# A graph layer's gather: fewer, wider register loads on SyncE, and more source columns copied by VectorE and ScalarE

## The chip, the cores and the metric

The kernel runs on one core of a Trainium2 chip. The metric is the device time of one execution in microseconds; what is compared is the median of several.

## The reference

A layer of a graph network with 12,500 nodes of 48 features and 400,000 edges, sorted by their destination. Every edge's message goes through two dense layers, and the messages are summed by destination:

```python
h = jnp.maximum(_layernorm(x, axis=-1), 0.0)
x_i, x_j = h[dst], h[src]
tmp = jnp.concatenate([x_i, x_j, edge_attr], axis=1)      # 48 + 48 + 32
hid = jax.nn.relu(tmp @ W1 + b1)                          # 128 wide
msg = hid @ W2 + b2
out = x + jax.ops.segment_sum(msg, dst, num_segments=12500)
```

All of it is in float32.

## The kernel before

A first part of some 70 us normalizes the nodes and multiplies them with the two halves of `W1`. That gives two tables with one row of 128 numbers for each node: `tab_a` for the destination (with the bias) and `tab_b` for the source, both in HBM. `tab_b` is also kept in SBUF, transposed, as `bt`: there a node is a column.

The edges are then worked off in 391 chunks of 1024, each of 8 tiles of 128 edges. For each chunk TensorE adds up, in PSUM (`pre`), the destination's row, the edge's attributes and the source's row. The first two come from one matmul per tile (line 409): since the edges are sorted, a chunk's destinations lie in a short run of nodes, so the left factor `lhs` holds a 0/1 matrix, which VectorE makes with one comparison (line 387, with a sum that goes to `deg` and is read out by a second instruction), and the right factor `rhs` holds the run's rows of `tab_a`. ScalarE then applies the ReLU (line 446, one activation a chunk, called `hid`). A second set of matmuls (line 456) sums the hidden values by destination, with the 0/1 matrix `hot` that VectorE makes (line 398), and VectorE adds the sums to a window of destinations, `seg` (line 471). Now and then the window moves on: VectorE clears and copies it (lines 487 and 489), and the old one is multiplied with `W2` and stored.

What bears on the change is how the source's rows get into `pre`. They can't be had by a comparison, since sources are random. There are three ways, and each of the 3125 tiles goes by one of them:

- By an indirect DMA of GpSimd, one instruction for each tile (line 379), from `tab_b` into `gb`, which has eight buffers of a chunk each. GpSimd starts with them before the loop and runs ahead as far as the buffers allow.
- By rows: SyncE reads the numbers of sources into its registers and issues one small DMA for each row (line 293). `RPART` = 15 rows a chunk make a tile in some eight and a half chunks.
- By columns: VectorE and ScalarE read numbers into their registers and copy one column of `bt` at a time into a tile `gt` (line 352), 128 instructions for a tile. TensorE multiplies such a tile by the identity and so turns it (line 430).

`PARTS` divides a chunk's columns into groups, each with its engine, its place in the strip `cols` of numbers and its size. The groups stand at fixed places of each engine's order: on VectorE the first follows the comparison of line 387, then come the second, the addition of line 471, the third, the comparison of line 398, and the fourth and fifth. For each group the engine first reads all its numbers by one register load (`numbers`, line 276), rounded up to a multiple of four, and then issues the copies. The second group's load also brings the address at which line 471 adds (`PLACE`). `tiles_of` works out how many tiles the columns make in all; the tiles that go by columns are not gathered by GpSimd.

SyncE's order in a chunk (`prepare`) is: the edges' attributes (line 362), the destinations (line 364), a register load of 16 numbers from `last` (the first destination, `BASE`, and 15 sources), the rows of `tab_a` (line 372) and the fifteen small DMAs of line 293.

Of the kernel before, what the change touches and what calls it, by code (L numbers as in the profile page):

```python
# [24 lines left out]
NCH = (NT + T - 1) // T  # L25
# [29 lines left out]
ROWS0 = 3  # L55
# [1 line left out]


PARTS = (
    (True, 0, 8), (True, 8, 15), (True, 24, 16), (True, 40, 20), (True, 60, 12),  # L60
    (False, 72, 12), (False, 84, 8), (False, 92, 8), (False, 100, 20), (False, 120, 12),
    (False, 132, 12),
)
PLACE = 23
STRIP = 144
PART = sum(n for _, _, n in PARTS)
SLOT = [at + k for _, at, n in PARTS for k in range(n)]
FIRST_OF = [sum(n for _, _, n in PARTS[:k]) for k in range(len(PARTS))]
RPART = 15
BASE = 0  # L70

BT0 = 16512
SEG0 = 165792
SEG_SIZE = 8 * L


AT_PLACE, AT_SEG, SEG, NEXT = 16, 17, 18, 19
WIDTH = 20
SLOTS = (NCH + 2 + P - 1) // P
BANK = 4  # L80

# [147 lines left out]
def windows(nc, tc, gp, bt, ident, idx, raw, rhss, x_t, tab_a, tab_b, dst, edge_t, w2s, b2s,  # L229
# [5 lines left out]
    with ExitStack() as es:  # L235
# [26 lines left out]
        st = {}  # L262
        gts = {}
        gss = {}

        def group(c):

            g = max(0, sum(first <= c for first in BEGINS) - 1)
            return g, c - BEGINS[g]
# [4 lines left out]
        def numbers(c, at, n, engine, table=last):  # L274

            return nc.values_load_multi_w_load_instructions(  # L276
                table[c % P : c % P + 1, c // P, at : at + n],
                engines=[engine], min_val=0, max_val=1 << 23,
                skip_runtime_bounds_check_because="numbers of nodes, and what is made of them",
            )[1]  # L280
# [48 lines left out]
        def columns(c, part):  # L329
# [5 lines left out]
            copy = nc.vector.tensor_copy if dve else nc.scalar.copy  # L335
            place = PLACE if at < PLACE <= at + PARTS[part][2] and c >= 2 else None
            size = -(-n // 4) * 4 if place is None else place + 1 - at
# [16 lines left out]
        def span(c):  # L354

            return next(w for w, last in SPANS if c < last)

        def prepare(c):
            n, w = min(T, NT - c * T), span(c)
            at = c * CE  # L360
            lhs = lhss[c % 3]
            nc.sync.dma_start(lhs[W:K, : n * P], edge_t[:, at : at + n * P])
            row = ld.tile([W, CE], I16, name="row")
            nc.sync.dma_start(
                row[:w, : n * P],
                dst[at : at + n * P].rearrange("(o e) -> o e", o=1).to_broadcast([w, n * P]),
            )
            m = max(0, min(RPART, len(BYROWS) * P - (c - ROWS0) * RPART)) if c >= ROWS0 else 0
            base, *nodes = numbers(c, BASE, 1 + m, mybir.EngineType.SP)
            rhs = rhss[c % 3]  # L370
            base = base.with_bounds(min_val=0, max_val=4 * HID * (N - 1))
            nc.sync.dma_start(
                rhs.bitcast(U8)[:w, :],
                taba8[bass.ds(base, 4 * HID * w)].rearrange("(w h) -> w h", w=w),
            )
            st[c] = dict(n=n, rows=nodes)
            gb = gp.tile([P, T, HID], F32, name="gb") if c >= RAW else None
            for t in range(n - len(COLS_OF.get(c, ())) - (c in BYROWS) if c >= RAW else 0):
                nc.gpsimd.indirect_dma_start(  # L379
                    out=gb[:, t, :], out_offset=None, in_=tab_b[:, :],  # L380
                    in_offset=bass.IndirectOffsetOnAxis(
                        ap=srci[:, c * T + t : c * T + t + 1], axis=0
                    ),
                )

            deg = degs[c % 3]
            nc.vector.tensor_scalar(  # L387
                lhs[:w, : n * P], row[:w, : n * P], bw[:w, c : c + 1], None,
                op0=ALU.is_equal, op1=ALU.add, accum_out=deg[:w, :1],
            )  # L390
            st[c].update(rhs=rhs, lhs=lhs, gb=gb, deg=deg)
# [70 lines left out]
        def add(c):  # L462

            s, w = st.pop(c), span(c)
            k = group(c)[0] % 2
            of = SEG0 + k * SEG_SIZE
            at = s["base"].with_bounds(
# [44 lines left out]
        with tc.manual_schedule():  # L512
            for c in range(NCH + 2):
                g, k = group(c - 2)
                if c < NCH:
                    prepare(c)
                    rows(c, st[c].pop("rows"))
# [173 lines left out]
def tile_gnn_preln(  # L691
# [31 lines left out]
    first = ctx.enter_context(tc.tile_pool(name="first", bufs=1))  # L723
# [28 lines left out]
    flag = const.tile([1, 1], I32, name="flag")  # L752
    last = const.tile([P, SLOTS, WIDTH], I32, name="last")
    cols = const.tile([P, SLOTS, STRIP], I32, name="cols")

# [7 lines left out]
    with tc.tile_pool(name="keep", bufs=1) as keep, tc.tile_pool(  # L763
# [82 lines left out]
        def check():  # L846

            p_c = ps_c.tile([1, P], F32, name="p_c")
            nc.tensor.transpose(p_c, furthest, ident)
            out_of = keep.tile([1, 1], F32, name="out_of")  # L850
            nc.vector.tensor_reduce(out_of, p_c, AX.X, ALU.max)
            nc.vector.tensor_scalar(flag, out_of, 0.5, None, op0=ALU.is_gt)

            nc.vector.tensor_scalar(bw, b0f[:W, :], wcol[:W, :], None, op0=ALU.add)

            nc.vector.tensor_scalar(cols, cols, 4, BT0, op0=ALU.mult, op1=ALU.add)
            rows_at = slice(BASE, BASE + 1 + RPART)
            nc.vector.tensor_scalar(
                last[:, :, rows_at], last[:, :, rows_at], 4 * HID, None, op0=ALU.mult
            )  # L860
            nc.vector.tensor_tensor(
                last[:, :, NEXT : NEXT + 1], last[:, :, NEXT : NEXT + 1],
                last[:, :, SEG : SEG + 1], op=ALU.subtract,
            )
            at = last[:, :, AT_PLACE : AT_PLACE + 1]
            nc.vector.scalar_tensor_tensor(
                at, last[:, :, AT_SEG : AT_SEG + 1], -4.0, at, op0=ALU.mult, op1=ALU.add
            )
            at_place = slice(PLACE, PLACE + 1)
            nc.vector.scalar_tensor_tensor(  # L870
                cols[:, :, at_place], cols[:, :, at_place], 1.0, at, op0=ALU.mult, op1=ALU.add
            )

        b0f = keep.tile([P, NCH], F32, name="b0f")
        node_tables(nc, tc, keep, x, ident, w1, b1, wb, ht, xg, ones, tab_a, tab_b, index, loads,
                    squares, most, check)
    outside = nc.values_load(flag[:1, :1], min_val=0, max_val=1)

    with tc.If(outside == 0) as cmp:
        windows(nc, tc, gp, bt, ident, (srci, rel, bw, wrow, last, cols, degs), (xg, wb, ht), rhss,  # L880
                x_t, tab_a, tab_b, dst16, edge_t, w2s, b2s, sources, out_t)
# [78 lines left out]
```

## Time and profile before

| | |
|---|---|
| median of 3 runs | 3349.78 us (3347.76 to 3354.19) |
| the profiled execution's own time | 3348.55 us |
| its span, first to last instruction | 3346.8 us |
| mean granted TensorE clock | 0.875 |
| tiles by GpSimd, by columns, by rows | 2650 (32 of them raw node rows before the loop), 430, 45 |

In the page's groups a row reads: line, engine, operation, what it writes and reads, count; then busy time in us and mean ns of one; then the idle time of the engine just before these instructions and what ended it. "issue" is idle time in which the engine waited for nothing that the profile shows. A row of a line's own view gives count, the shortest, median and longest duration in ns, and the first and last start. A row by stretches gives the stretch, its length, the engine's busy time with the count in brackets, the granted clock, the DMA share and GB/s. A row of the waits gives who waited for whom, us in total, times, and the longest. A row of the timeline gives start, duration, engine, line and operation, with the idle time before it in brackets. Register loads are done by an engine's sequencer (DVEq, SPq, ACTq) and do not count as busy time of the engine.

### The profile page before, as it was taken

Reading aid. Unit: us, or ns where it says so; the run is one execution under the profiler, and the core shown is the slowest. Engines: PE = TensorE matmul, PEld = TensorE weight load, DVE = VectorE, ACT = ScalarE, POOL = GpSimd, SP = SyncE. Lnnn points to the kernel's source line nnn. Section 1 sums busy time; section 2 is a strip of 40 time slices with the busy share of each in tenths; the row PEclk is TensorE's granted clock in tenths of the full one; section 3 lists DMA queues with packets and bytes.
Section 4 is the critical chain, followed back from the end, with each engine's and each line's share of the span. In section 5 each row is a group of like instructions: output and inputs, shape, how many; then the busy total and the mean of one; then the engine's idle time right before and its main releaser. Section 6 shows DMA issues by size and latency. Waiting matters only on the chain.

```text
span 3346.8 us, 114800 instructions
## 1 busy us (share of the span) xinstructions
PE 2804.1 (84%) x16242; PEld 2228.4 (67%) x16242; DVE 2608.9 (78%) x29052; ACT 3044.9 (91%) x28183; POOL 2516.1 (75%) x2672
## 2 busy tenths in 40 slices
PE   7988888888888888888888888888877888788877
PEld 6676767666666676766666676666665666666655
DVE  6477777777777777788777777887878788888886
ACT  5799999999999998999999999999999999999997
POOL 7777777777777777777777777777777777777776
PEclk9988888888888888888888888998989888899898
DMA  7322223233333333333333333333333333333332
GB/s 259 110 77 78 77 77 78 76 80 83 84 83 82 83 82 83 84 89 88 86 86 88 87 88 85 93 91 93 93 93 93 93 90 93 96 100 98 100 98 76
DMA packets 171145, 307.66 MB, mean 92 GB/s; under 512 B 68611, under 2 KB 93813, under 8 KB 169093
## 3 DMA queue, kind: packets, MB, share of 16 engines
q0 software_dynamic: 84800, 172.53, 20.7%
q1 hardware_dynamic: 85170, 127.53, 12.7%
q14 instruction: 634, 5.19, 0.5%
q8 instruction: 137, 2.24, 0.3%
q10 hardware_dynamic: 404, 0.17, 0.0%
HBM read 284.21 MB, written 18.34 MB: 90 GB/s over the span
## 4 chain that ended last, share of the span: by engine, by line
DVE 34%; POOL 25%; issue 22%; PE 10%; ACT 4%; DMA 3%; DVEq 2%; ACTq 0%; SPq 0%; POOLq 0%
POOL gb L379 25%; DVE gt L352 25%; DVE lhs L387 6%; ACT gt L352 3%; DMA gb<-tab_b,srci 3%; PE pre L409 3%; PE pre L430 2%; PE p_g L456 2%; DVE hot L398 2%; DVEq L276 2%; PE p_n L194 1%; ACT hid L446 1%; DVE seg L471 1%; PE pre L306 0%; ACTq L276 0%
## 5 line engine op out<-in xcount | busy, mean ns | idle before, releaser
L379 POOL DMA_INDIRECT gb<-tab_b,srci x2618 | 2476.4, 946 | 805.3 <-issue 759.8
L352 ACT COPY gt<-bt 128x1 f32 x27705 | 2619.5, 188 | 76.6 <-issue 66.1
L352 DVE COPY gt<-bt 128x1 f32 x27335 | 1839.8, 143 | 616.7 <-issue 578.7
L430 PE MATMUL pre<-gb,ident 128*128 128x512 f32 (+2 forms) x1548 | 851.7, 668 | 234.9 <-DMA gb<-tab_b,srci 227.7
L409 PEld LDWEIGHTS pre<-rhs,lhs 112*128 112x128 f32 x6250 | 888.6, 220 | 187.0 <-issue 118.4
L409 PE MATMUL pre<-rhs,lhs 112*128 112x128 f32 x6250 | 884.3, 302 | 27.5 <-issue 17.1
L456 PE MATMUL p_g<-hot,hid 128*128 128x64 f32 (+4 forms) x6250 | 789.9, 279 | 111.2 <-ACT hid L446 109.2
L456 PEld LDWEIGHTS p_g<-hot,hid 128*128 128x128 f32 x6250 | 769.0, 200 | 139.7 <-ACT hid L446 138.8
L430 PEld LDWEIGHTS pre<-gb,ident 128*128 128x128 f32 x1548 | 314.3, 234 | 536.1 <-issue 469.0
L446 ACT ACTIVATE hid<-pre 128x1024 f32<-128x1024 f32 x391 | 397.7, 1017 | 175.4 <-PE pre L430 158.5
L387 DVE TENSOR_SCALAR_CACHE_REDUCE lhs<-row,bw 64x1024 f32<-64x1024 int16 (+4 forms) x391 | 492.2, 1259 | 3.0 <-DMA row<-in_dst 3.0
L430 PE MATMUL pre<-ident,gt 128*128 128x128 f32 x860 | 224.2, 349 | 137.9 <-DVE gt L352 118.8
L430 PEld LDWEIGHTS pre<-ident,gt 128*128 128x128 f32 x860 | 148.6, 217 | 157.6 <-issue 77.6
L398 DVE TENSOR_TENSOR hot<-wnum,rel 128x512 f32<-128x512 f32 (+4 forms) x391 | 207.0, 529 | 0.0
L459 PE MATMUL p_g<-ident,deg 80*128 80x32 f32 (+4 forms) x782 | 159.7, 286 | 0.0
L471 DVE TENSOR_TENSOR seg<-seg,p_g 128x128 f32 (+4 forms) x391 | 94.1, 241 | 80.6 <-PE p_g L459 79.9
L459 PEld LDWEIGHTS p_g<-ident,deg 80*128 80x128 f32 x782 | 128.3, 206 | 0.0
L499 PE MATMUL p_f<-seg,w2s 128*48 128x512 f32 (+1 forms) x58 | 35.9, 705 | 5.5 <-DVE xseg L506 5.1
L773 POOL DMA_INDIRECT xg<-in_x,srci x32 | 31.0, 967 | 10.2 <-issue 8.8
L500 PE MATMUL p_f<-seg,b2s 1*48 1x512 f32 (+1 forms) x58 | 33.3, 656 | 0.0
L203 ACT COPY tab<-p_n 128x512 f32<-128x512 f32 x33 | 18.7, 584 | 12.1 <-PE p_n L194 11.8
L387 DVE DVE_READ_ACCUMULATOR lhs<-row,bw 64x1 f32 (+4 forms) x391 | 28.8, 74 | 0.0
(78 smaller groups left out, 357.7 us busy)
## 6 DMA issues: line engine op xcount, KB each, us to landing
gs<-tab_b SPq DMA_DIRECT2D x5760, 0.5 KB
lhs<-in_edge_t SPq DMA_DIRECT2D x390, 128.0 KB
gb<-tab_b,srci POOLq DMA_INDIRECT x2618
row<-in_dst SPq DMA_DIRECT2D x90, 128.0 KB
row<-in_dst SPq DMA_DIRECT2D x85, 96.0 KB
row<-in_dst SPq DMA_DIRECT2D x50, 160.0 KB
row<-in_dst SPq DMA_DIRECT2D x87, 64.0 KB
tab_b<-tab SPq DMA_DIRECT2D x3, 1280.0 KB
```

The lines of the kernel that those rows point to most:

```text
L276: return nc.values_load_multi_w_load_instructions(table[c % P : c % P + 1, c // P, at : at + n], engines=[engine], min_val=0, max_val=1 << 23,
L352: copy(gts[j][:, e : e + 1], bt8[:, bass.ds(of, 4)].bitcast(F32))
L379: nc.gpsimd.indirect_dma_start(out=gb[:, t, :], out_offset=None, in_=tab_b[:, :], in_offset=bass.IndirectOffsetOnAxis(ap=srci[:, c * T + t ...
L387: nc.vector.tensor_scalar(lhs[:w, : n * P], row[:w, : n * P], bw[:w, c : c + 1], None, op0=ALU.is_equal, op1=ALU.add, accum_out=deg[:w, :1],)
L398: nc.vector.tensor_tensor(hot[:, :n, :], wnum[:, :w].unsqueeze(1).to_broadcast([P, n, w]), rel[:, c * T : c * T + n].unsqueeze(2).to_broad ...
L409: nc.tensor.matmul(pre[:, t, :], s["lhs"][:K, t * P : (t + 1) * P], s["rhs"][:K, :], start=t % BANK == 0, stop=False, skip_group_check=True,)
L430: nc.tensor.matmul(pre[:, t:e, :], lhsT, rhs, start=False, stop=True, skip_group_check=True)
L446: nc.scalar.activation(h[:, :n, :], s["pre"][:, :n, :], AF.Relu)
L456: nc.tensor.matmul(p_g[:, 0, :], s["h"][:, t, :], s["hot"][:, t, :], start=t == 0, stop=t == n - 1)
L459: nc.tensor.matmul(p_g[:, 1, :], s["deg"], ident[:W, :w], start=True, stop=True)
L471: nc.vector.tensor_add(to, to, s["p_g"])
L499: nc.tensor.matmul(p_f[:, :n], w2s, seg[:, 0, s], start=True, stop=False)
```

## The change

VectorE's groups are 12, 15, 16, 20 and 9 columns instead of 8, 15, 16, 20 and 12, one column more in all (72 for 71). ScalarE's last group is 14 instead of 12 (74 for 72). Together 146 columns a chunk are copied instead of 143. SyncE loads 32 numbers (two chunks' 15 sources and two first destinations) in every even chunk, and uses the second half in the next one. The strips become wider to match.

```diff
 PARTS = (
-    (True, 0, 8), (True, 8, 15), (True, 24, 16), (True, 40, 20), (True, 60, 12),
-    (False, 72, 12), (False, 84, 8), (False, 92, 8), (False, 100, 20), (False, 120, 12),
-    (False, 132, 12),
+    (True, 0, 12), (True, 12, 15), (True, 28, 16), (True, 44, 20), (True, 64, 9),
+    (False, 76, 12), (False, 88, 8), (False, 96, 8), (False, 104, 20), (False, 124, 12),
+    (False, 136, 14),
 )
-PLACE = 23
-STRIP = 144
+PLACE = 27
+STRIP = 152
...
-BASE = 0
+BASE = 2 * RPART
...
-AT_PLACE, AT_SEG, SEG, NEXT = 16, 17, 18, 19
-WIDTH = 20
+AT_PLACE, AT_SEG, SEG, NEXT = 32, 33, 34, 35
+WIDTH = 36
...
+        ahead = []
...
-            base, *nodes = numbers(c, BASE, 1 + m, mybir.EngineType.SP)
+            if c % 2 == 0:
+                ahead[:] = numbers(c, 0, 2 * RPART + 2, mybir.EngineType.SP)
+            base, nodes = ahead[BASE + c % 2], ahead[c % 2 * RPART :][:m]
...
-            rows_at = slice(BASE, BASE + 1 + RPART)
+            rows_at = slice(0, BASE + 2)
```

More of the change, by code (lines that the diff above doesn't have):

```diff
@@ L69 @@
 RPART = 15
-BASE = 0
+BASE = 2 * RPART
 BT0 = 16512
-SEG0 = 165792
+SEG0 = 166176
 SEG_SIZE = 8 * L
-AT_PLACE, AT_SEG, SEG, NEXT = 16, 17, 18, 19
-WIDTH = 20
+AT_PLACE, AT_SEG, SEG, NEXT = 32, 33, 34, 35
+WIDTH = 36
 SLOTS = (NCH + 2 + P - 1) // P
@@ L908 @@
     numbers[2 : NCH + 2, AT_PLACE] = SEG0 + of % 2 * SEG_SIZE - BT0
-    numbers[:NCH, BASE] = first
+    bases = np.pad(first, (0, -NCH % 2)).reshape(-1, 2)
+    numbers[: NCH + NCH % 2 : 2, BASE : BASE + 2] = bases
     numbers[:NCH, SEG] = seg
@@ L920 @@
     rows = by_tile[in_rows].reshape(-1)
-    rows = np.pad(rows, (0, -len(rows) % RPART)).reshape(-1, RPART)
-    numbers[ROWS0 : ROWS0 + len(rows), BASE + 1 : BASE + 1 + RPART] = rows
+    by_chunk = np.zeros((NCH + NCH % 2) * RPART, np.int32)
+    by_chunk[ROWS0 * RPART : ROWS0 * RPART + len(rows)] = rows
+    numbers[: NCH + NCH % 2 : 2, : 2 * RPART] = by_chunk.reshape(-1, 2 * RPART)
     last = np.ascontiguousarray(numbers.reshape(SLOTS, P, WIDTH).transpose(1, 0, 2))
```

## The prediction

> **What bounds the kernel now.** I read the page first: busy shares, then the costliest groups.
>
> ```profile
> PE 2804.1 (84%) x16242; PEld 2228.4 (67%) x16242; DVE 2608.9 (78%) x29052; ACT 3044.9 (91%) x28183; POOL 2516.1 (75%) x2672
> ...
> L379 POOL DMA_INDIRECT gb<-tab_b,srci x2618 | 2476.4, 946 | 805.3 <-issue 759.8
> L352 ACT COPY gt<-bt 128x1 f32 x27705 | 2619.5, 188 | 76.6 <-issue 66.1
> L352 DVE COPY gt<-bt 128x1 f32 x27335 | 1839.8, 143 | 616.7 <-issue 578.7
> ```
>
> By busy share ScalarE is the fullest engine and GpSimd the emptiest. That is misleading: GpSimd's idle time is nearly all "issue", it waits for nobody. So I asked next for the GpSimd gathers (line 379) by stretches, and for where they begin and end.
>
> ```profile
> 200.00:700.00 500.00, 377.71 (x402) 0.86 0.30 77
> 700.00:1500.00 800.00, 604.84 (x641) 0.85 0.32 83
> 1500.00:2500.00 1000.00, 756.41 (x800) 0.87 0.34 89
> 2500.00:3300.00 800.00, 605.14 (x640) 0.90 0.36 96
> ```
>
> ```profile
> L379 POOL DMA_INDIRECT gb<-tab_b,srci x2618: 940/944/1774, 52.6 to 3331.6; - x187
> ```
>
> The counts say one gather per 1.25 us in every stretch (800/641, 1000/800, 800/640), from 52.6 to 3331.6: 2618 x 1.25 = 3272 of these 3279 us. GpSimd never stops. It gathers 2618/387 = 6.76 tiles per chunk, 8.44 us. Now the pace of the chunks themselves, by ScalarE's one activation per chunk (line 446) in the same stretches:
>
> ```profile
> 200.00:700.00 500.00, 63.02 (x62) 0.86 0.30 77
> 700.00:1500.00 800.00, 99.65 (x98) 0.85 0.32 83
> 1500.00:2500.00 1000.00, 120.18 (x118) 0.87 0.34 89
> 2500.00:3300.00 800.00, 96.81 (x95) 0.90 0.36 96
> ```
>
> Up to 1500 us a chunk takes 8.06 to 8.16 us, less than GpSimd's 8.44: the chunks catch up with a lead that GpSimd has from starting at 52.6. From 1500 on a chunk takes 8.42 to 8.47, GpSimd's own pace. The waits say the same. Below are TensorE's longest wait before 1500 and after, then VectorE's wait for TensorE's sums, before and after:
>
> ```profile
> PE pre L430 <- DVE gt L352: 82.2, 79, 2.7
> ```
>
> ```profile
> PE pre L430 <- DMA gb<-tab_b,srci: 227.7, 150, 3.4
> ```
>
> ```profile
> DVE seg L471 <- PE p_g L459: 3.0, 1, 3.0
> ```
>
> ```profile
> DVE seg L471 <- PE p_g L459: 49.4, 27, 4.4
> ```
>
> Early, TensorE waits for VectorE's copied columns and VectorE for nobody: VectorE sets the 8.1 us. Late, TensorE waits for gathers and VectorE idles 49.4 us in all. So GpSimd sets the end, and VectorE is a close second with some 50 us to spare. What fills VectorE's 8.1 us is not its 78% of busy time. Its register loads (line 276) and the timeline of one chunk show it:
>
> ```profile
> L276 DVEq TENSOR_LOAD <-cols x1: 1101/1101/1101, 401.7 to 401.7; - x1
> L276 DVEq TENSOR_LOAD <-cols x1: 1351/1351/1351, 403.4 to 403.4; - x1
> L276 DVEq TENSOR_LOAD <-cols x1: 846/846/846, 405.4 to 405.4; - x1
> L276 DVEq TENSOR_LOAD <-cols x1: 596/596/596, 406.8 to 406.8; - x1
> L276 DVEq TENSOR_LOAD <-cols x1: 1100/1100/1100, 407.7 to 407.7; - x1
> L276 DVEq TENSOR_LOAD <-cols x1: 1107/1107/1107, 409.4 to 409.4; - x1
> ```
>
> ```profile
> 402.02 0.18 DVE L471 TENSOR_TENSOR seg<-seg,p_g 128x32 f32 x1
> 402.84 1.06 DVE L352 COPY gt<-bt 128x1 f32 x16 [0.64 <-issue]
> 403.82 0.28 DVE L398 TENSOR_TENSOR hot<-wnum,rel 128x128 f32<-128x128 f32 x1
> 404.80 1.30 DVE L352 COPY gt<-bt 128x1 f32 x20 [0.69 <-issue]
> 406.34 0.82 DVE L352 COPY gt<-bt 128x1 f32 x12 [0.24 <-issue]
> 407.07 1.26 DVE L387 TENSOR_SCALAR_CACHE_REDUCE lhs<-row,bw 16x1024 f32<-16x1024 int16 x1
> 408.27 0.07 DVE L387 DVE_READ_ACCUMULATOR lhs<-row,bw 16x1 f32 x1
> ```
>
> The five loads are those for 16, 20, 12, 8 and 16 numbers: 0.85 - 0.60 = 0.25 us for four numbers. From 401.7 to 409.4 is 7.7 us; the loads hold the sequencer for 5.0 of them, and the other 2.7 go to sending out some 76 instructions, 0.036 each. (After the load that ends at 402.80 the next starts at 403.4: 0.6 us for sixteen copies and the comparison.) The sequencer is never free: it is the resource, and the "issue" idle of line 352 is its loads.
>
> **The change part by part.** *GpSimd.* 146 columns a chunk for 143 make 385 x 146 / 128 = 439 tiles by column instead of 430, so nine gathers go: 9 x 1.25 = 11.2 us, all of it on the path that sets the end now.
>
> *ScalarE* gets two copies: 2619.5 / 27705 = 0.095 us each, 0.19 a chunk, 73 us over 385 chunks, and four more numbers in its last load, about 0.25 by VectorE's rows, sent while earlier copies still run. What hides it:
>
> ```profile
> ACT hid L446 <- PE pre L430: 158.5, 141, 9.8
> ```
>
> ScalarE waits 158.5 us for TensorE; 73 fit. If that cover were gone, up to 73 + 385 x 0.25 = 169 us could show; below nothing it cannot go. I take 0.
>
> *TensorE* multiplies nine more tiles in single form:
>
> ```profile
> L430 PE MATMUL pre<-ident,gt 128*128 128x128 f32 x860 | 224.2, 349 | 137.9 <-DVE gt L352 118.8
> ```
>
> Two of 0.35 us a tile make 6 us at most, beside its waits: 0.
>
> *SyncE* now loads 32 numbers in every second chunk for 16 in each.
>
> ```profile
> L276 SPq TENSOR_LOAD <-last x421: 275/1192/1482, 76.0 to 3330.4; - x141
> ```
>
> ```profile
> SPq L362 <- PE pre L409: 127.2, 83, 5.3
> ```
>
> No row has a load of 32. It lies between 1.19 (the median, nearly all of them for 16) and 2.38 (twice that); from 0.275 for one number to 1.19 for 16 is 0.061 a number, which gives 2.17, the value I take. So SyncE saves 0.1 us a chunk, and in even chunks the rows behind the load (line 372's and the fifteen of line 293) go out 1 us later, in odd ones 1.2 earlier. SyncE waits 127.2 us for buffers that TensorE still reads, so it runs ahead as far as these allow, and neither shows: 0. Uncovered, 1 us in 196 even chunks would be 196 us. The wider strips make two scalings before the loop longer, by 32 and 64 elements a partition; line 398 does 128 in 0.28 us, so under 0.3 us once.
>
> *VectorE.* Loads grow from 8+16+16+20+12 numbers to 12+16+16+20+12, since nine are rounded up to twelve: +0.25 us. One more copy is sent: +0.04. That is 0.29 a chunk on the engine that has none to spare. The new order adds to it. Count from the end of the last group's load (405.4 + 0.846 = 406.25). Now: twelve copies and the comparison of line 387 are sent by 406.8, the load for eight ends at 407.4, eight copies are sent, and the next load starts at 407.7, 1.45 after the count began. After: nine copies and line 387 take 0.44, the load for twelve 0.85, together 1.29, and twelve copies would be out by 1.75. But do they fit into the queue? Line 387 starts when nine copies have run, at 0.09 + 9 x 0.061 = 0.64 (twelve took 0.73: 406.34 to 407.07), and holds the datapath for 1.20 (to 408.27): until 1.84. How many wait in front of a busy datapath is seen where line 487's clearing holds it:
>
> ```profile
> L276 DVEq TENSOR_LOAD <-cols x1: 1122/1122/1122, 1559.7 to 1559.7; - x1
> ```
>
> ```profile
> L276 DVEq TENSOR_LOAD <-cols x1: 1389/1389/1389, 1562.0 to 1562.0; - x1
> ```
>
> ```profile
> 1560.77 0.84 DVE L487 MEMSET seg<- 128x944 f32 x1
> 1561.54 0.18 DVE L489 COPY seg<-seg 128x160 f32 x1
> 1561.63 0.50 DVE L352 COPY gt<-bt 128x1 f32 x7
> ```
>
> The last row is cut at the second load's start. The same sixteen copies and comparison that took 0.6 us above take 1562.0 - 1560.8 = 1.2 here, and when the sequencer gets to its next load, seven copies have started: nine copies and the comparison wait, ten in all. With ten places, line 387's read of its accumulator and nine copies fill the queue; the twelfth copy is sent when the second has started, at 1.84 + 0.06, and the load starts one sending later, 0.04, at 1.94. That is 1.94 - 1.45 = 0.49 us a chunk, and the three copies fewer in the last group are in it. (Today's eight and the accumulator read are nine: they just fit.)
>
> [...]
>
> Sum: 385 x 0.49 = 189 us. Against it stands what VectorE idles now, which goes once GpSimd is ahead again: 49.4 + 3.0 us in 28 waits. The sequencer stands some 0.3 to 0.4 us longer in each (the load at 401.7 begins 0.3 before the addition at 402.02 does), and waits too short to empty the queue don't show: an estimate of 68 us. So +121 us on the profiled execution, 3348.55 us (its span is 3346.8), which is 1.2 under the median 3349.78: the forecast is 3470 us. The 11.2 us of GpSimd bring nothing, since it is then the engine that waits.
>
> **The rivals.** *The queue takes all twelve.* Then only load and copy count: 385 x 0.29 = 112, less 68: 3394 us. Against it is the held sequencer at 1560.8; for it, that the clearing is another instruction than line 387. [...] *GpSimd stays the bound, faster.* If a chunk costs VectorE less than 68/385 = 0.18 us more, its idle time swallows it and the nine gathers show: 3339 us. It would need loads that get cheaper than the 0.25 for four numbers, for instance because SyncE's load less often meets VectorE's; SyncE reads as many numbers as before, and the rows of one size agree within 7 ns, which speaks against it. *The waits stay:* if TensorE keeps VectorE waiting as now, 189 are added in full, 3538 us; the early stretch, where GpSimd is ahead and VectorE waits 3.0 us in all, speaks against it.
>
> **How the numbers follow.** Forecast 0.73, all twelve 0.13, eight or waits that stay 0.07, faster 0.07. The forecast's own range, 3440 to 3500, comes from 0.45 to 0.55 us a chunk and 55 to 75 us of idle time regained. With the first rival the range is 3390 to 3500; outside it lie 0.14 and the forecast's ends. A measurement of this kernel can tell about 0.2% from no change: faster by more than that 0.06, within it 0.01, slower 0.93.
>
> **What would show it.** Right: 2609 gathers with pauses for buffers that TensorE reads, not one per 1.25 us; TensorE's wait for gathers near zero in all stretches; 8.6 us a chunk before 1500; VectorE's wait at line 471 a few us; the load behind the first group starting just after that group's second copy, about 0.1 after line 387 ends. If it starts while line 387 runs, the queue is deeper; if ScalarE's line 446 stops waiting for TensorE, ScalarE is the bound and I am wrong; if gathers still come every 1.25 us to the end, the faster rival holds.

## The result and the profile after

| | before | changed |
|---|---|---|
| median of 5 runs | 3347.98 us | 3478.59 us |
| ratio, 95% interval | | 1.0389 (1.0378 to 1.0401) |
| span of the profiled execution | 3346.8 us | 3476.9 us |

The change costs 131 us; 121 were forecast. In eight of the experiments below, called paused runs there, the kernel before took 5406 or 5488 us (medians) beside them, for a cause that no run shows (with SyncE's loads alone VectorE and ScalarE got out two or three instructions per 1.43 us from 2001.7 to 2007.4 us, while GpSimd's gathers still came every 1.25 us up to 2004.9), so that only single undisturbed chunks are read from those runs.

The changed kernel's lines stand a little further down: 276 is now 277, 352 is 353, 379 is 382, 387 is 390, 430 is 433, 446 is 449, 459 is 462 and 471 is 474; runs built on the kernel before keep its numbers. First the line of each page that gives the shares, by engine, of the chain of work that ended last, before and then after, the latter with the same groups as above:

```profile
DVE 34%; POOL 25%; issue 22%; PE 10%; ACT 4%; DMA 3%; DVEq 2%; ACTq 0%; SPq 0%; POOLq 0%
```

```profile
DVE 66%; issue 21%; PE 4%; ACT 4%; DVEq 4%; ACTq 0%; DMA 0%; SPq 0%
...
L382 POOL DMA_INDIRECT gb<-tab_b,srci x2609 | 2468.3, 946 | 883.5 <-issue 743.1
L353 ACT COPY gt<-bt 128x1 f32 x28472 | 2719.9, 187 | 90.5 <-issue 70.0
L353 DVE COPY gt<-bt 128x1 f32 x27720 | 1862.2, 143 | 760.1 <-issue 750.7
```

Nine gathers are gone, as worked out, and GpSimd's share of the chain went with them: from 25% to nothing that shows (POOL is GpSimd). VectorE's idle time marked "issue" grew from 578.7 to 750.7 us. Next, the pace of the chunks by stretches (line 449, one activation a chunk):

```profile
200.00:700.00 500.00, 58.97 (x58) 0.84 0.29 75
700.00:1500.00 800.00, 94.60 (x93) 0.84 0.31 80
1500.00:2500.00 1000.00, 118.00 (x116) 0.85 0.33 87
2500.00:3300.00 800.00, 92.94 (x92) 0.88 0.35 92
```

That is 8.6 us a chunk (500/58, 800/93, 1000/116) and 8.7 at the end (800/92), where the kernel before had 8.1 and then 8.4. The gathers, with what GpSimd waited for:

```profile
L382 POOL DMA_INDIRECT gb<-tab_b,srci x2609: 938/945/1840, 52.4 to 3401.9; - x187
...
  issue: 743.1, 2420
  PE pre L433: 108.1, 93
```

The last gather goes out at 3401.9, 75 us ahead of the end (before: 15 us), and GpSimd now waits 108.1 us for TensorE to free its buffers. The waits of TensorE and VectorE, first from 150 to 1500 us (where none of line 474 shows) and then after 1500:

```profile
PE pre L433 <- DVE gt L353: 130.8, 89, 3.4
...
PE pre L433 <- DMA gb<-tab_b,srci: 1.6, 1, 1.6
```

```profile
DVE seg L474 <- PE p_g L462: 18.8, 6, 5.5
...
PE pre L433 <- DVE gt L353: 178.2, 110, 4.2
...
PE pre L433 <- DMA gb<-tab_b,srci: 5.6, 4, 2.2
```

TensorE hardly waits for gathers any longer (227.7 us before, 7.2 now) but for VectorE's columns, both before and after 1500 us. One chunk on VectorE: the loads for the last group, the first and the second, and the timeline, cut where the third load starts.

```profile
L277 DVEq TENSOR_LOAD <-cols x1: 846/846/846, 405.1 to 405.1; - x1
L277 DVEq TENSOR_LOAD <-cols x1: 849/849/849, 406.4 to 406.4; - x1
L277 DVEq TENSOR_LOAD <-cols x1: 1098/1098/1098, 407.9 to 407.9; - x1
```

```profile
406.00 0.64 DVE L353 COPY gt<-bt 128x1 f32 x9 [0.24 <-issue]
406.55 1.26 DVE L390 TENSOR_SCALAR_CACHE_REDUCE lhs<-row,bw 16x1024 f32<-16x1024 int16 x1
407.75 0.07 DVE L390 DVE_READ_ACCUMULATOR lhs<-row,bw 16x1 f32 x1
407.75 0.20 DVE L353 COPY gt<-bt 128x1 f32 x2
```

The first group's load ends at about 407.2. Twelve copies take 0.43 us to send, at the prediction's 0.036 each, and could be out by 407.7. But the next load starts at 407.9, when the comparison of line 390 is over and two copies have started (two in 310 of the 380 chunks between 150 and 3440 us, three to five in the others). From the last group's load (its end at 405.95) that is 1.95 us; 1.94 was forecast. The chunk is no exception: over all chunks of the trace this stretch has a median of 1.96 us, and 1.47 in the kernel before.

### The profile page after: what moved, and what is told of

It reads as the page before. It is cut to its first block, busy times and chain, and to the rows that moved or that the text cites. A ratio compares the mean times of both kernels' runs of the same rounds, so it can differ in the third digit from the quotient of the medians.

```text
span 3476.9 us, 115820 instructions
## 1 busy us (share of the span) xinstructions
PE 2845.0 (82%) x16260; PEld 2256.9 (65%) x16260; DVE 2629.4 (76%) x29437; ACT 3139.6 (90%) x28950; POOL 2508.0 (72%) x2663
## 4 chain that ended last, share of the span: by engine, by line
DVE 66%; issue 21%; PE 4%; ACT 4%; DVEq 4%; ACTq 0%; DMA 0%; SPq 0%
DVE gt L353 47%; DVE lhs L390 12%; DVE hot L401 5%; DVEq L277 4%; ACT gt L353 3%; DVE seg L474 2%; PE p_n L194 1%; PE pre L412 1%; PE p_g L459 1%; ACT hid L449 1%; PE pre L307 0%; DVE seg L490 0%; DVE xseg L509 0%; PE pre L433 0%; ACTq L277 0%
## 5 line engine op out<-in xcount | busy, mean ns | idle before, releaser
L353 ACT COPY gt<-bt 128x1 f32 x28472 | 2719.9, 187 | 90.5 <-issue 70.0
L353 DVE COPY gt<-bt 128x1 f32 x27720 | 1862.2, 143 | 760.1 <-issue 750.7
L412 PEld LDWEIGHTS pre<-rhs,lhs 112*128 112x128 f32 x6250 | 875.8, 218 | 278.8 <-issue 181.8
L449 ACT ACTIVATE hid<-pre 128x1024 f32<-128x1024 f32 x391 | 397.4, 1016 | 196.2 <-PE pre L433 181.6
L433 PEld LDWEIGHTS pre<-gb,ident 128*128 128x128 f32 x1548 | 347.8, 248 | 275.7 <-issue 275.0
L433 PE MATMUL pre<-ident,gt 128*128 128x128 f32 x878 | 243.7, 367 | 345.5 <-DVE gt L353 311.0
L433 PEld LDWEIGHTS pre<-ident,gt 128*128 128x128 f32 x878 | 159.1, 227 | 375.7 <-issue 205.8
```

What stands on the lines that cost most here:

```text
L353: copy(gts[j][:, e : e + 1], bt8[:, bass.ds(of, 4)].bitcast(F32))
L412: nc.tensor.matmul(pre[:, t, :], s["lhs"][:K, t * P : (t + 1) * P], s["rhs"][:K, :], start=t % BANK == 0, stop=False, skip_group_check=True,)
L433: nc.tensor.matmul(pre[:, t:e, :], lhsT, rhs, start=False, stop=True, skip_group_check=True)
L449: nc.scalar.activation(h[:, :n, :], s["pre"][:, :n, :], AF.Relu)
```

## The experiments

In all of them the places in the strips follow the groups' sizes. Two theories of the loss stood against each other. By the first it is VectorE's sequencer: four numbers and one copy more in each chunk, and besides them a queue of ten that holds the sequencer back when twelve copies stand behind the comparison. By the second, numbers and copies alone count, or ScalarE or SyncE has a part.

**Ten copies first.** The changed kernel with the same numbers loaded and the same 72 columns, only otherwise divided between the first and the last group.

```diff
-    (True, 0, 12), (True, 12, 15), (True, 28, 16), (True, 44, 20), (True, 64, 9),
+    (True, 0, 10), (True, 12, 15), (True, 28, 16), (True, 44, 20), (True, 64, 11),
```

> The changed kernel with VectorE's groups in the order 10, 15, 16, 20, 11, again the same numbers and copies. Queue of ten: ten copies and the accumulator's read are eleven, the last one waits for the end of the comparison, which two copies more in the last group make later than with twelve first. The load behind the first group starts at 2.00 us, 0.05 later than in the changed kernel: 3478 + 385 x 0.05 = 3497 us. So between nine and ten copies the time jumps by 100 us. Work alone counts: 3478 us, as with nine. A queue that is some places longer: 3398 us, as with nine.

That was a paused run, 5533 us (1.0089 of the kernel before), but its undisturbed chunks, with the 1.74 us that the next expectation gives, already contradicted the 2.00. It was run again:

> The kernel with VectorE's groups in the order 10, 15, 16, 20, 11 once more, for its time in a state in which the kernel before takes its 3348 us: in the earlier call all sequencers paused for stretches and the kernel before took 5488. The chunks between the pauses showed the load behind the first group start 1.74 us after the end of the last group's load, so ten copies fit beside the accumulator's read, which takes no place. If the held sequencer is 0.21 us a chunk of the loss: 3478 - 385 x 0.21 = 3397 us. If the loss is loads and copies alone: 3478 us.

Measured 3415.39 us, 1.0173 of before (1.0155 to 1.0191). That is 18 above the 3397, with the kernel before at 3354 beside it. One chunk's three loads, and the timeline, cut shortly after the third begins:

```profile
L277 DVEq TENSOR_LOAD <-cols x1: 847/847/847, 399.0 to 399.0; - x1
```

```profile
L277 DVEq TENSOR_LOAD <-cols x1: 849/849/849, 400.4 to 400.4; - x1
```

```profile
L277 DVEq TENSOR_LOAD <-cols x1: 1095/1095/1095, 401.6 to 401.6; - x1
```

```profile
400.62 1.26 DVE L390 TENSOR_SCALAR_CACHE_REDUCE lhs<-row,bw 16x1024 f32<-16x1024 int16 x1
401.82 0.07 DVE L390 DVE_READ_ACCUMULATOR lhs<-row,bw 16x1 f32 x1
401.82 0.20 DVE L353 COPY gt<-bt 128x1 f32 x2
```

The load behind the first group starts at 401.6, while the comparison still runs: all ten copies were sent by then, and none had started, nor had the accumulator's read. The ten counted behind line 487's clearing (seven of the sixteen copies started at the next load in eight of 13 such places of that trace, eight in the other five) had no such read among them, for the comparison there is line 398. So ten places fit both, and what was wrong in the expectation is that the accumulator's read takes one. With twelve copies both ways of counting let the last one go when the second starts, which is why the forecast of the changed kernel came out all the same. The order alone is worth 1.0389 - 1.0173, some 72 us, or 0.19 us a chunk (0.21 expected).

**Nine copies first.** The same with 9 and 12.

```diff
-    (True, 0, 12), (True, 12, 15), (True, 28, 16), (True, 44, 20), (True, 64, 9),
+    (True, 0, 9), (True, 12, 15), (True, 28, 16), (True, 44, 20), (True, 64, 12),
```

> The changed kernel with VectorE's groups in the order 9, 15, 16, 20, 12: the first and the last exchanged, so the same 76 numbers are loaded and the same 72 columns copied. Queue of ten: nine copies and the accumulator's read are ten, they all fit while line 387's comparison runs, and the load behind them starts 1.73 us after the end of the last group's load, not 1.94. That is 0.21 us a chunk less, 385 x 0.21 = 81, so 3398 us. Work alone counts (the loss is numbers and copies, or comes from the other engines): nothing is saved, 3478 us. [...]

A paused run, 5530 us; the ratio of 1.0074 says nothing of the 3398. In an undisturbed chunk:

```profile
L277 DVEq TENSOR_LOAD <-cols x1: 866/866/866, 407.0 to 407.0; - x1
```

```profile
L277 DVEq TENSOR_LOAD <-cols x1: 1133/1133/1133, 409.7 to 409.7; - x1
```

```profile
408.73 1.26 DVE L390 TENSOR_SCALAR_CACHE_REDUCE lhs<-row,bw 16x1024 f32<-16x1024 int16 x1
409.92 0.07 DVE L390 DVE_READ_ACCUMULATOR lhs<-row,bw 16x1 f32 x1
409.92 0.38 DVE L353 COPY gt<-bt 128x1 f32 x5
```

From 407.9 to 409.7 are 1.8 us (1.73 expected), and the comparison is running: all nine copies are sent and none has started, as with ten.

**Twelve first in the kernel before.** The same 71 columns and 72 numbers as before, in the order 12, 15, 16, 20, 8.

```diff
-    (True, 0, 8), (True, 8, 15), (True, 24, 16), (True, 40, 20), (True, 60, 12),
+    (True, 0, 12), (True, 12, 15), (True, 28, 16), (True, 44, 20), (True, 64, 8),
```

> The kernel before with VectorE's groups in the order 12, 15, 16, 20, 8: the same 72 numbers and 71 columns as before. Queue of ten: the comparison runs until 1.78 us after the end of the last group's load, the twelfth copy waits for it, and the next load starts at 1.88; with the 0.25 that the last group's smaller load saves, a chunk costs 1.88 - 0.25 - 1.45 = 0.18 us more. 385 x 0.18 = 69 us, which is just what VectorE idled: 3348 to 3356 us, with line 471's waits for TensorE almost gone and 8.3 us a chunk before 1500 us instead of 8.1. Work alone counts: 3348 us, 8.1 us a chunk and the waits as before.

A paused run, 5403.73 us, 1.0002 (0.9991 to 1.0013): the forecast on time and waits was not tested. An undisturbed chunk:

```profile
L276 DVEq TENSOR_LOAD <-cols x1: 607/607/607, 409.9 to 409.9; - x1
```

```profile
L276 DVEq TENSOR_LOAD <-cols x1: 1132/1132/1132, 412.4 to 412.4; - x1
```

```profile
411.12 1.26 DVE L387 TENSOR_SCALAR_CACHE_REDUCE lhs<-row,bw 16x1024 f32<-16x1024 int16 x1
412.31 0.07 DVE L387 DVE_READ_ACCUMULATOR lhs<-row,bw 16x1 f32 x1
412.31 0.20 DVE L352 COPY gt<-bt 128x1 f32 x2
```

With twelve first the load waits here too until two copies have started (412.4, some 1.9 us after the last group's load; 1.88 expected), in a kernel that loads no number and copies no column more.

**Loads of exactly as many numbers as are used.**

```diff
-            size = -(-n // 4) * 4 if place is None else place + 1 - at
+            size = n if dve and place is None else -(-n // 4) * 4 if place is None else place + 1 - at
```

VectorE's groups are 8, 15, 16, 20 and 13 with it, 72 columns as in the changed kernel. First a paused run (5535.54 us, 1.0077), then again:

> The changed kernel with VectorE's groups 8, 15, 16, 20, 13, and VectorE's loads no longer rounded up to fours, so the fifth brings 13 numbers: one number and one copy a chunk more than before, and the same 439 tiles by column as in the changed kernel. If a load is priced by the number (0.0625 us) and a copy by its sending (0.036), that is 385 x 0.10 = 38 us, less than the 68 that VectorE idled; GpSimd stays the bound and shows nine gathers fewer: 3337 us. If a load of 13 costs as much as one of 16: 385 x 0.29 - 68 = 44 us, 3392 us.

> The changed kernel with VectorE's groups 8, 15, 16, 20, 13 and its loads no longer rounded up to fours, once more, for its time without the pauses. One number (0.0625 us) and one copy (0.036) a chunk more on VectorE than before are 385 x 0.10 = 38 us, less than the 68 it idled: GpSimd stays the bound and shows nine gathers fewer, 3348 - 11 = 3337 us. If a load of 13 costs as much as one of 16: 3392 us.

Measured 3406.87 us, 1.0179 (1.0164 to 1.0193): the price by the number was wrong, and the time lies 15 us above the 3392 for the other price too. The load for 13 numbers, after the last group's place in a chunk:

```profile
L277 DVEq TENSOR_LOAD <-cols x1: 1097/1097/1097, 406.9 to 406.9; - x1
```

It takes what one for 16 takes (1100). So for 13, the one size of a group's load tried here that is no multiple of four, the whole four is paid whether the kernel rounds up or not, and a 72nd column on VectorE costs it. With eight copies first (in the kernel before the load behind them starts at 407.7, the comparison ends at 408.3) this run is at the same time the changed kernel without anything held: its 61 us are the part of the loss that loads and sending make, after what VectorE's idle time takes up.

**VectorE's old groups in the changed kernel.** ScalarE's 74 columns and SyncE's loads stay.

```diff
-    (True, 0, 12), (True, 12, 15), (True, 28, 16), (True, 44, 20), (True, 64, 9),
+    (True, 0, 8), (True, 8, 15), (True, 24, 16), (True, 40, 20), (True, 60, 12),
```

First a paused run (5532.14 us, 1.0084), then again:

> The changed kernel with VectorE's old groups 8, 15, 16, 20, 12; ScalarE's 74 columns and SyncE's loads for two chunks stay. 145 columns a chunk make 436 tiles, so six gathers fewer than before. VectorE alone is the cause: GpSimd sets the end again and shows its six gathers, 3348 - 6 x 1.25 = 3340 us. ScalarE's copies or SyncE's late rows have a part in the loss: above 3348, and 3410 if it is half.

> The changed kernel with VectorE's old groups 8, 15, 16, 20, 12, once more, for its time without the pauses; ScalarE's 74 columns and SyncE's loads for two chunks stay, six gathers fewer than before. VectorE alone is the cause of the loss: 3348 - 7.5 = 3340 us. ScalarE or SyncE has a part in it: above 3348.

Measured 3340.49 us, 0.998 of before (0.9971 to 0.9989). The whole loss lies in VectorE's groups, and what is left of the change is a version faster than both kernels: 5.5 us less than before, where six gathers fewer are worth 7.5. The last gather stands 13 us ahead of the end of its span, 3334.1 (15 before), and TensorE's wait for gathers is back (after 1500 us):

```profile
L382 POOL DMA_INDIRECT gb<-tab_b,srci x2612: 940/944/1787, 52.2 to 3321.2; - x187
```

```profile
PE pre L433 <- DMA gb<-tab_b,srci: 214.0, 142, 3.4
```

**Single parts of the change in the kernel before.** Three runs, SyncE's loads alone, ScalarE's columns alone and VectorE's groups alone; each has one of these three pieces of the change.

```diff
-            base, *nodes = numbers(c, BASE, 1 + m, mybir.EngineType.SP)
+            if c % 2 == 0:
+                ahead[:] = numbers(c, 0, 2 * RPART + 2, mybir.EngineType.SP)
+            base, nodes = ahead[BASE + c % 2], ahead[c % 2 * RPART :][:m]
...
-    (False, 132, 12),
+    (False, 132, 14),
...
-    (True, 0, 8), (True, 8, 15), (True, 24, 16), (True, 40, 20), (True, 60, 12),
+    (True, 0, 12), (True, 12, 15), (True, 28, 16), (True, 44, 20), (True, 64, 9),
```

> The kernel before with SyncE's loads for two chunks alone. Off the path, as forecast: within 0.2% of before, 3348 us; one load of 2.1 us in even chunks, none in odd ones. Rows that go out 1 us later in even chunks reach VectorE or TensorE late: up to 196 us slower.

> The kernel before with ScalarE's 74 columns alone: 436 tiles by column, six gathers fewer. ScalarE's 0.19 us a chunk are hidden in its waits: 3348 - 7.5 = 3340 us. If its cover is too thin, up to 73 us slower and its wait for TensorE near zero.

> The kernel before with VectorE's groups 12, 15, 16, 20, 9 alone. VectorE alone is the cause: the whole loss is there, 3475 to 3480 us. ScalarE's and SyncE's parts have a share: clearly below 3470.

All three were paused runs: 1.0008 (0.9996 to 1.0019), 1.011 (1.0091 to 1.0129) and 1.0028 (1.0014 to 1.0043) of a kernel before that took 5406 us. They are inconclusive for its 3348 us. The run with the old groups answers the question of the three as far as it goes: SyncE's and ScalarE's parts together cost nothing that shows while GpSimd sets the end.

**Two more columns on ScalarE**, on top of the exact loads.

```diff
-    (False, 76, 12), (False, 88, 8), (False, 96, 8), (False, 104, 20), (False, 124, 12),
-    (False, 136, 14),
+    (False, 76, 12), (False, 88, 8), (False, 96, 8), (False, 104, 20), (False, 124, 14),
+    (False, 140, 14),
```

> The exact loads with two more columns on ScalarE (last groups 14 and 14, 76 in all): 148 columns a chunk, 445 tiles, fifteen gathers fewer than before. If ScalarE's waits of 158 us cover its four copies more (385 x 0.38 = 146 us) and VectorE has some 30 us left: 3348 - 19 = 3329 us. If ScalarE becomes the bound, its wait for TensorE goes to nearly zero and the time is above 3340 us.

Measured 3413.4 us, 1.02 (1.0186 to 1.0214). The forecast rests on the load of 13 that turned out to cost a four, so VectorE was the bound, and the 3329 was not tested. What it shows is ScalarE's wait for TensorE, which went to

```profile
ACT hid L449 <- PE pre L433: 43.0, 50, 6.5
```

from 158.5 in the kernel before and 127.4 with the exact loads alone. A fifth copy, at 385 x 0.095 = 37 us, would take nearly all of it; that is an estimate.

## Why the prediction was right, and where its sum was off

The bound changed as forecast: from GpSimd's steady gathers to VectorE's sequencer. The step with the queue held in the numbers (1.95 us for 1.94) and nearly in the time: of the 131 us the order makes some 70 (131 less the 61 of the exact loads, or 72 by ten first), forecast 385 x 0.20 = 77. Of one detail it was wrong: the accumulator's read takes no place among the ten.

That the sum came within 10 us is partly luck, for two of its terms were off in opposite directions. The pace of VectorE's comparisons, one a chunk, shows it. Before 1500 us, where VectorE hardly waits for TensorE, here are the kernel before, the exact loads and the changed kernel:

```profile
L387 DVE TENSOR_SCALAR_CACHE_REDUCE lhs<-row,bw x160: 1256/1257/1267, 204.2 to 1499.6; 32x1024 f32<-32x1024 int16 x87, 16x1024 f32<-16x1024 int16 x63, 48x1024 f32<-48x1024 int16 x10
```

```profile
L390 DVE TENSOR_SCALAR_CACHE_REDUCE lhs<-row,bw x155: 1256/1257/1265, 198.8 to 1494.8; 32x1024 f32<-32x1024 int16 x87, 16x1024 f32<-16x1024 int16 x64, 48x1024 f32<-48x1024 int16 x4
```

```profile
L390 DVE TENSOR_SCALAR_CACHE_REDUCE lhs<-row,bw x152: 1256/1257/1268, 200.6 to 1497.5; 32x1024 f32<-32x1024 int16 x87, 16x1024 f32<-16x1024 int16 x64, 48x1024 f32<-48x1024 int16 x1
```

Divided by 159, 154 and 151 steps that is 8.15, 8.42 and 8.59 us a chunk. So loads and sending cost 0.27 (priced at 0.29), the held sequencer 0.17 (0.20), together 0.44 and not 0.49: 385 x 0.44 = 169 us instead of 189. In the median the stretch from the last group's load to the second group's grew by the forecast 0.49, in the mean over the chunks by 0.45 only (1.54 to 1.99): on the longest tenth of these stretches less came on top (it begins at 1.82 us before and 2.11 after, 0.29 apart).

With 169 us added and 131 lost, 38 were swallowed and not 68. This term, the idle time that VectorE would get back, is the one that was most mis-sized, by some 30 us. After 1500 us, before and then after:

```profile
L387 DVE TENSOR_SCALAR_CACHE_REDUCE lhs<-row,bw x214: 1257/1261/1274, 1499.6 to 3298.8; 64x1024 f32<-64x1024 int16 x45, 48x1024 f32<-48x1024 int16 x38, 80x1024 f32<-80x1024 int16 x24
```

```profile
L390 DVE TENSOR_SCALAR_CACHE_REDUCE lhs<-row,bw x207: 1257/1261/1274, 1505.8 to 3296.7; 64x1024 f32<-64x1024 int16 x45, 48x1024 f32<-48x1024 int16 x42, 80x1024 f32<-80x1024 int16 x17
```

A chunk took 8.45 us there in the kernel before, 0.30 more than early; over some 215 chunks that is 64 us, so the idle time itself was estimated well. But the changed kernel still takes 8.69 there, 0.10 more than early, and so keeps some 22 us of it. Line 474's six long waits for TensorE, 18.8 us, which the forecast had let go ("a few us"), are most of these. The two errors, -20 and +30, make the 10 us between 121 and 131.

SyncE and ScalarE were put at nothing, and nothing shows: the old groups with both left in are faster than before, and with both in, the exact loads' 0.27 us a chunk leaves no room for them beside VectorE's own 0.29. SyncE's load of 32 was put at 2.17 us:

```profile
L277 SPq TENSOR_LOAD <-last x226: 282/2111/2420, 75.7 to 3456.1; - x113
```

Its median, 2.11, is a little less. ScalarE waits for TensorE even longer than before, 181.6 us for 158.5, in spite of 100 us more of copies (2719.9 for 2619.5; 73 were forecast). TensorE's own waits for VectorE's columns (311.0 us by the page, 118.8 before) may explain it; no run tests that. With the old groups, where GpSimd sets the end again, the two copies do use up cover:

```profile
ACT hid L449 <- PE pre L433: 59.6, 81, 4.6
```

The rivals: all twelve fitting (3394 us), waits that stay in full (3538 us) and GpSimd staying the bound (3339 us) are refuted by the changed kernel's 3479 us and its traces. No run shows the eight that has a share in the chances: with ten copies first the load behind them starts at 401.6, before the first of them does (401.82), so none of the ten was held.

## What to carry to other kernels

An engine that is busy 78% of the time may have no time left: add up its sequencer's register loads and the sending of its instructions (here 5.0 and 2.7 us), and compare the sum with the period (7.7 us). Short instructions behind a long one should be no more than can wait there: here ten copies were all sent while a comparison of 1.26 us ran, and with twelve the next load started only when two of them had, 1.96 us after the last group's load instead of 1.47 with eight. Work that is shifted to relieve the bound has to be priced at the receiving engine's true resource; here nine gathers of 1.25 us were bought with 385 loads that grew by 0.25 and a sequencer held for 0.17 more in each chunk.

## What the hardware showed that was not expected

Behind a running comparison ten copies of VectorE waited, all sent (the next load at 401.6 us, the first copy at 401.82); the accumulator's read waited there too (401.82), so with ten places it takes none of them. A register load of 13 numbers took as long as one of 16, 1.097 us and 1.100, where 12 took 0.846.
